# Another table of places for the order of all instructions in a graph stack of four layers

## The chip, the cores and the metric

The kernel runs on one core of a Trainium2 chip. The metric is the device time of one launch in microseconds (us). A core has engines with an instruction stream each: PE (TensorE, matrix products into PSUM), DVE (VectorE), ACT (ScalarE), POOL (GpSimd) and SP (SyncE, which here issues nearly all DMAs). [...]

## The reference

`x` is 32 graphs of 512 nodes with 256 features, `adj` their 0/1 adjacency. Four layers follow each other, each on a normalised and clipped copy of x. Everything is float32.

```python
h = relu(layernorm(x)); x = x + gat4(h, adj)       # layer 0: 4 heads of 64, exp(leaky(e_i + e_j)), softmax over j
h = relu(layernorm(x)); x = x + gat1(h, adj)       # layer 1: 1 head of 256, softmax over i
h = relu(layernorm(x)); x = x + edge(h, adj)       # layer 2: scores (h * a_0) h^T, leaky, softmax
h = relu(layernorm(x)); x = x + transformer(h, adj)  # layer 3: 8 heads of 32, Wo, norm, 256-1024-256 net, norm
```

## The kernel before

**One list of jobs for each graph.** `quick_path` (line 325) walks through the 32 graphs. For each it makes two loads (`adj`, `x`), then `masks`, `layer0` to `layer3`. These functions issue nothing yet: each operation is handed to a plan (`plan.dve`, `plan.act`, `plan.matmuls`, `plan.dma`), which appends a job. There are 497 jobs to a graph, in the same order for every graph.

**The table decides the order.** A job's place is the graph's number times 100,000 plus the table's entry for that job's position in the list (`put`, line 150). `carry_out` (line 178) sorts the jobs of all graphs by place and issues them in that order. On each engine this order is kept; across engines the data decide. The entries are keys for a sort and no times.

```python
place = self.number * ROUND + self.table[self.at] if self.place is None else self.place
```

Entries reach to almost 500,000, so five graphs are under way at once. I call the leading digit of an entry its stage (0 to 4), and round r the jobs with places from r times 100,000: in round r graph r is in stage 0, graph r-1 in stage 1, and so on to graph r-4 in stage 4. Rounds 0 to 3 fill this pipeline, rounds 4 to 31 are full, rounds 32 to 35 drain it.

**What the stages hold.** Roughly: stage 0 has loads, the mask, layer 0's normalisation and first products (`ps_t`, `ps_wh`, `ps_sp`); stage 1 layer 0's four heads (`p` on DVE, `ps_o` on PE); stage 2 layer 1 and most of layer 2; stage 3 the end of layer 2 and layer 3's `ps_qk`, `ps_v` and attention; stage 4 layer 3's `ps_wo` and feed-forward net (`ps_f`).

**The attention of layer 3** (lines 695 to 724) goes in eight steps, two groups of four heads by four blocks of keys. A step is: four score products (`ps_s`, contraction over 32 rows), two exponentials on ACT (`p<-ps_s`), one multiplication by the mask on DVE (`p<-p,m`), and eight products into 32 columns each (`ps_ct` for the context, `ps_to` for the row sums). The buffer `p3` holds two steps.

**Buffers.** A tile takes the slot of its kind that was used longest ago. PSUM has two slots for layers 0 to 2 and the last net (`ps_a`), two for layer 3 (`ps_b`), and one each for `ps_ct` and `ps_to`. `p` has 6 slots, `mT` 3. The layer weights are loaded on POOL's queue behind the load of the first x (`plan.load`, line 238), at the place that `plan.aside(max(PLACES[:2]) + 1)` gives.

Of the kernel before, what the change touches and what calls it, by code (L numbers as in the profile page):

```python
# [56 lines left out]
class Part:  # L57


    def __init__(self, home, rows, index, steps=()):  # L60
        self.home, self.rows, self.index, self.steps = home, rows, index, steps
# [61 lines left out]
class Plan:  # L123
# [8 lines left out]

    def __init__(self, tc, table):
        self.tc, self.nc, self.table = tc, tc.nc, table
        self.jobs = []

    def graph(self, number):

# [136 lines left out]
def width(args):  # L275
# [4 lines left out]

ROUND = 100000
PLACES = [
    19807, 0, 43241, 57619, 64598, 73580, 81389, 88138, 134062, 235662, 143142, 287307, 285553, 232853, 15635,
    15811, 28841, 27985, 23993, 15811, 30374, 30229, 32369, 32370, 32370, 32446, 32844, 48496, 34324, 44230,
    44177, 46695, 46041, 50344, 54161, 54792, 54792, 54792, 51041, 51777, 57310, 57310, 57310, 57738, 57738,
    57832, 57739, 58104, 61341, 61341, 67966, 61898, 61898, 67567, 69254, 72469, 69482, 77323, 74000, 76325,
    79818, 78024, 78024, 80713, 80713, 80714, 82170, 88138, 93984, 93675, 88138, 100363, 101562, 103520,
    103520, 103520, 103520, 99026, 98456, 107942, 108892, 114155, 115978, 115979, 116955, 117229, 118109,
    112967, 112266, 118498, 118106, 122333, 124077, 124856, 124856, 126720, 126720, 130323, 126361, 126793,
    124647, 132760, 132760, 132760, 132760, 134221, 134221, 134221, 134221, 134221, 134727, 134221, 156322,  # L290
    140191, 134912, 142057, 169073, 157725, 170057, 172384, 201862, 202787, 205641, 207797, 208539, 176096,
    208573, 211867, 216328, 218484, 218484, 219056, 219056, 219056, 219056, 219056, 218484, 218484, 218484,
    218484, 218485, 227052, 227119, 228253, 219613, 219613, 220424, 224906, 224906, 228631, 223683, 224122,
    224122, 229201, 229201, 232797, 231582, 232020, 232794, 233389, 243904, 244480, 249048, 254893, 242125,
    242231, 243790, 254173, 237217, 238008, 241105, 245079, 237839, 238826, 242604, 256707, 257566, 258334,
    259006, 259006, 259006, 259519, 259519, 259519, 259519, 259519, 392456, 255868, 267182, 259006, 259006,
    259892, 259665, 259006, 259006, 259892, 259665, 266786, 266786, 268621, 269711, 273176, 302934, 273176,
    273176, 273176, 277010, 277447, 281097, 281097, 281195, 281196, 281196, 281682, 281682, 281682, 281682,
    281683, 281196, 281683, 282840, 282840, 284327, 283254, 286775, 286821, 286821, 287236, 288036, 287335,
    282681, 282681, 283122, 282681, 284575, 293213, 293213, 295654, 291792, 291574, 293905, 297714, 297584,  # L300
    297714, 298819, 298819, 297714, 287489, 287489, 290592, 290231, 298206, 300033, 308229, 310297, 310297,
    303799, 303799, 303799, 305379, 305380, 306132, 308300, 312883, 316207, 394029, 437737, 327509, 328548,
    327753, 325228, 328998, 329876, 332238, 330645, 332238, 332502, 332502, 332608, 332717, 364575, 332717,
    332717, 332717, 332717, 332717, 338203, 340406, 340406, 340406, 340407, 340407, 340905, 341309, 341309,
    352943, 347109, 352371, 352371, 353369, 353369, 353417, 354661, 356381, 356381, 356381, 357144, 357399,
    346769, 348254, 348493, 351248, 352029, 352189, 352199, 352199, 352554, 359237, 359237, 359237, 359237,
    364034, 360298, 360301, 360448, 365688, 377452, 366095, 368722, 368232, 374829, 379739, 379671, 380891,
    379672, 382370, 383191, 386847, 392755, 392755, 387818, 392756, 395158, 396303, 407857, 382331, 382331,
    382615, 382634, 388690, 385894, 388773, 389314, 389314, 394131, 390806, 394842, 396200, 401293, 405927,
    398693, 403322, 398865, 403593, 407530, 409955, 410479, 412422, 412422, 408793, 409986, 423530, 354795,  # L310
    408893, 410479, 418263, 418263, 418263, 419191, 419191, 419191, 419191, 419128, 417119, 437177, 437347,
    419191, 420203, 420203, 420203, 420203, 420721, 420203, 420203, 421199, 422452, 422452, 423633, 423633,
    432009, 424134, 424134, 424718, 424718, 424759, 425616, 425916, 425916, 425916, 425916, 426698, 426841,
    426841, 426970, 427475, 430939, 430939, 427202, 428368, 428368, 428368, 429763, 429360, 431209, 431243,
    432263, 432263, 432291, 432540, 430070, 430071, 430071, 430071, 430446, 430071, 431829, 432836, 432836,
    435307, 436332, 440746, 435945, 435945, 436252, 436626, 436626, 437927, 444318, 444318, 444811, 444811,
    444811, 445291, 445291, 445291, 445291, 445447, 445572, 436110, 437653, 437653, 437653, 437653, 437653,
    438770, 440843, 440843, 440843, 440843, 440843, 440872, 442233, 442446, 442446, 442446, 445600, 445600,
    442446, 442446, 445601, 445601, 442446, 442704, 446845, 449648, 449758, 449759, 449759, 454221, 449777,
    450699, 450699, 450699, 450699, 450699, 450699, 491710,  # L320
]


# [993 lines left out]
```

## Time and profile before

| | us |
|---|---|
| median of 3 runs (3751.09 to 3758.95) | 3752.26 |
| the profiled execution | 3758.1 |
| its span, first to last instruction | 3756.2 |
| PE busy in the span | 3635.0 (97%) |
| DVE busy | 2732.6 (73%) |
| ACT busy | 1803.8 (48%) |
| one full round (graph to graph) | 111.37 |

In the profile all planned operations have one line each for their helper: L214 for DVE and ACT, L259 for PE's matmuls, L257 for its transposes. So groups are told apart by tile names. Names have their numbers left out: `ps_o` is the head product of layer 0 (65 columns), the product of layer 1 (256) and that of layer 2 (257); `ps_f` are both products of the net. Every float32 matmul is two instructions on PE, a transpose is one.

### The profile page before, as it was taken

What the parts mean: (1) busy time and instruction counts of PE and PEld (TensorE: products, weight loads), DVE (VectorE), ACT (ScalarE), POOL (GpSimd) and SP (SyncE); (2) the same over time, 40 slices, a digit from 0 to 9 for tenths busy, and PEclk for the clock granted to TensorE, in tenths of its full rate; (3) what the DMA queues carried; (4) which work ended last, traced back from release to release, by engine and by line L of the source; (5) the groups of instructions that cost most, each with busy time, mean ns of one, the idle gap of its engine ahead of it and who ended that gap; (6) DMA issues with size and microseconds to landing.
All of it is one profiled execution on the core that took longest, in us unless ns stands there. A gap on an engine that the chain in (4) does not pass through costs nothing.

```text
span 3756.2 us, 51774 instructions
## 1 busy us (share of the span) xinstructions
PE 3635.0 (97%) x19974; PEld 2366.4 (63%) x19974; DVE 2732.6 (73%) x6267; ACT 1803.8 (48%) x3393; POOL 11.1 (0%) x25
## 2 busy tenths in 40 slices
PE   4799999999999999999999999999999999999996
PEld 4666766666766666666666666666666666666553
DVE  4577777877777777777787777787777777777653
ACT  1245445555444555444555544555544455544543
POOL 1000000000000000000000000000000000000000
PEclk7599999999999999999999999999999999999998
DMA  4111111111111111011111111111111111100000
GB/s 120 57 32 33 36 49 46 43 42 36 29 49 46 43 49 36 23 47 47 49 43 38 40 29 49 46 43 49 29 29 49 46 43 49 38 29 27 15 9 11
DMA packets 152349, 152.72 MB, mean 41 GB/s; under 512 B 87840, under 2 KB 122144, under 8 KB 148000
## 3 DMA queue, kind: packets, MB, share of 16 engines
q1 hardware_dynamic: 149632, 144.35, 13.8%
q0 software_dynamic: 1216, 3.94, 0.3%
q8 instruction: 159, 2.61, 0.3%
q10 hardware_dynamic: 1248, 1.05, 0.1%
q14 instruction: 94, 0.77, 0.1%
HBM read 114.57 MB, written 17.96 MB: 35 GB/s over the span
## 4 chain that ended last, share of the span: by engine, by line
PE 95%; DVE 3%; ACT 1%; DMA 1%; issue 1%; SPq 0%; ACTq 0%; DVEq 0%
PE ps_o L259 25%; PE ps_f L259 24%; PE ps_s L259 7%; PE ps_ct L259 7%; PE ps_wh L259 6%; PE ps_qk L259 6%; PE ps_to L259 6%; PE ps_e L259 4%; PE ps_t L257 4%; PE ps_v L259 3%; PE ps_wo L259 3%; DVE p L214 1%; PE ps_y L257 1%; DVE st L214 0%; DMA mT<-m 0%
## 5 line engine op out<-in xcount | busy, mean ns | idle before, releaser
L259 PE MATMUL ps_o<-wh,p 128*128 128x65 f32 (+1 forms) x5120 | 750.5, 303 | 30.2 <-DVE p L214 24.6
L259 PEld LDWEIGHTS ps_o<-wh,p 128*128 128x128 f32 x5120 | 705.6, 200 | 102.7 <-issue 60.5
L214 DVE TENSOR_TENSOR p<-p,m 128x2048 f32<-128x2048 f32 x256 | 582.7, 2286 | 29.7 <-ACT p L214 29.6
L214 ACT ACTIVATE p<-ps_s 128x1024 f32<-128x1024 f32 x512 | 501.2, 1022 | 208.1 <-PE ps_s L259 205.3
L259 PE MATMUL ps_f<-tT,ff_t 128*128 128x512 f32 x1024 | 462.7, 602 | 1.7 <-ACT tT L214 1.7
L259 PE MATMUL ps_f<-ff_t,f 128*128 128x256 f32 x2048 | 461.0, 379 | 0.0
L259 PEld LDWEIGHTS ps_f<-ff_t,f 128*128 128x128 f32 x2048 | 381.9, 190 | 64.0 <-issue 15.3
L214 DVE SCALAR_TENSOR_TENSOR p<-rows,rt,mT 128x512 f32<-128x512 f32 x512 | 370.1, 735 | 16.7 <-DMA mT<-m 16.7
L214 ACT ACTIVATE h<-x,shift,rstd 128x256 f32<-128x256 f32 x512 | 268.6, 595 | 152.8 <-PE ps_o L259 106.3
L259 PEld LDWEIGHTS ps_f<-tT,ff_t 128*128 128x128 f32 x1024 | 189.4, 192 | 229.3 <-issue 188.7
L259 PE MATMUL ps_s<-qk 32*128 32x512 f32 x2048 | 294.2, 640 | 1.3 <-ACT qk L214 0.8
L259 PE MATMUL ps_ct<-p,v 128*32 128x512 f32 x2048 | 272.0, 603 | 9.3 <-DVE p L214 6.3
L214 ACT ACTIVATE f<-ps_f,ff1b_c 128x512 f32<-128x512 f32 x256 | 164.8, 682 | 235.7 <-PE ps_f L259 235.7
L259 PE MATMUL ps_to<-p,ones 128*32 128x512 f32 x2048 | 266.6, 592 | 0.0
L259 PE MATMUL ps_qk<-h3T,wqkv_t 128*128 128x512 f32 x512 | 239.1, 594 | 0.0
L259 PE MATMUL ps_o<-h,p 128*128 128x257 f32 x1024 | 239.0, 385 | 0.0
L259 PEld LDWEIGHTS ps_o<-h,p 128*128 128x128 f32 x1024 | 190.1, 191 | 51.5 <-issue 26.0
L214 DVE BATCH_NORM_STATS2 st<-x 128x6 f32<-128x256 f32 x512 | 195.6, 415 | 6.8 <-DMA x<-in_x_dram 4.7
L214 ACT ACTIVATE rstd<-mv,eps 128x4 f32<-128x4 f32 x192 | 56.4, 294 | 298.6 <-DVE mv L214 286.0
L257 PE MATMUL ps_t<-ident,h 128*128 128x128 f32 x1024 | 172.6, 281 | 25.0 <-ACT h L214 17.6
L259 PEld LDWEIGHTS ps_s<-qk 32*128 32x128 f32 x2048 | 81.3, 182 | 164.6 <-ACT y L214 78.0
L257 PEld LDWEIGHTS ps_t<-ident,h 128*128 128x128 f32 x1024 | 130.8, 145 | 85.2 <-issue 52.3
(131 smaller groups left out, 4322.9 us busy)
## 6 DMA issues: line engine op xcount, KB each, us to landing
adj<-in_adj_dram SPq DMA_DIRECT2D x32, 1024.0 KB
rows<-rows_d SPq DMA_DIRECT2D x32, 1024.0 KB
x<-in_x_dram SPq DMA_DIRECT2D x32, 512.0 KB
rows<-rows_d SPq DMA_DIRECT2D x32, 512.0 KB
out_dram<-y SPq DMA_DIRECT2D x32, 512.0 KB
inv<-in_d SPq DMA_DIRECT2D x32, 256.0 KB
ff_t<-in_L_gnn_W_dram POOLq DMA_DIRECT2D x2, 1024.0 KB, 12.5
mT<-m SPq DMA_TRANSPOSE x128
```

The costliest lines, as they stand in the source:

```text
L214: return [getattr(unit, method)(*map(real, args), **{k: real(v) for k, v in kw.items()})]
L257: made.append(self.nc.tensor.transpose(*map(real, c)))
L259: made.append(self.nc.tensor.matmul(*map(real, c[:3]), start=c[3], stop=c[4]))
```

## The change

The table `PLACES` (lines 282 to 321) is replaced; 496 of its 497 entries differ. The plan's constructor also gets `number = None`, which changes no instruction. The jobs, their operands, their buffers' kinds and slot counts are the same.

```diff
-        self.jobs = []
+        self.jobs, self.number = [], None
...
 PLACES = [
-    19807, 0, 43241, 57619, 64598, 73580, 81389, 88138, 134062, 235662, 143142, 287307, 285553, 232853, 15635,
...
-    450699, 450699, 450699, 450699, 450699, 450699, 491710,
+    4941, 0, 45989, 55878, 52736, 53088, 65883, 75806, 126827, 257141, 153885, 318759, 211656, 217633, 19570,
...
+    442345, 444396, 453835, 453835, 478083,
 ]
```

What moves, read from the two tables:

- 39 jobs change their stage. Layer 0's first head (four `ps_o` jobs, their release on DVE and three further `p`) goes from stage 1 to 0. The root and shift of layer 1's normalisation go from 2 to 1, three of the four `ps_o` jobs of layer 2 from 3 to 2, the last two attention steps from 4 to 3. Three small DVE jobs move on by a stage or two.
- The cyclic order of a full round stays alike. PE before: first head, two layer-2 `ps_o`, `ps_ct` of steps 7 and 8, two `ps_o`, `ps_wo` with the second head inside. After: three matmul jobs of the first head, `ps_y`, the fourth, one layer-2 `ps_o`, `ps_ct` of steps 7 and 8, three `ps_o`, the second head, `ps_wo`.
- Layer 1's `ps_wh`: before, eight jobs in five runs between single jobs of the third head; after, four jobs, then the whole third head, then two, one and one between the transposes of layer 3's first norm.
- Between those transposes (`ps_t<-ident,n`) and the first `ps_f` PE had two `ps_wh` jobs; now it has two jobs of the fourth head.
- In attention, `ps_t` of layer 2 moves from behind `ps_ct` of step 3 to in front of it, and `ps_e` and `ps_y` of layer 2 stand in other gaps.
- On DVE, the four `p` of a head: before, two of them stood behind the release of the head in front (second, third and fourth head alike); now two, three and two do, and in the second and fourth head the first one that PE uses is the last one made.
- On SP, three of the four mask transposes (`mT<-m`) now stand in front of the store of layer 0's row (`rows_d`), before two did. The load of adj stands directly behind that of x, now by 4,941 places, before by 19,807; nothing else of SP lies between in either table for the first graph.

## The prediction

> **What bounds the kernel now.** I read the page first: span, busy shares, chain.
>
> ```profile
> span 3756.2 us, 51774 instructions
> PE 3635.0 (97%) x19974; PEld 2366.4 (63%) x19974; DVE 2732.6 (73%) x6267; ACT 1803.8 (48%) x3393; POOL 11.1 (0%) x25
> PEclk7599999999999999999999999999999999999998
> PE 95%; DVE 3%; ACT 1%; DMA 1%; issue 1%; SPq 0%; ACTq 0%; DVEq 0%
> ```
>
> PE carries the end: 95% of the chain. Its clock is low in the first two slices only. Next the busy times by round. I found the round from the first head's product, which comes back every 111.37 us. Columns: stretch, length, then busy time and count of PE, PEld, DVE, ACT, POOL; clock; DMA.
>
> ```profile
> 96.00:138.40 42.40, 37.72 (x153) 34.19 (x153) 16.21 (x40) 4.86 (x14) 0.00 (x0) 0.50 0.10 36
> 184.50:273.60 89.10, 84.55 (x475) 55.97 (x476) 64.17 (x153) 42.16 (x80) 0.00 (x0) 0.90 0.09 25
> 273.60:384.98 111.38, 111.38 (x627) 72.40 (x626) 84.96 (x196) 56.22 (x107) 0.00 (x0) 1.00 0.15 42
> 3280.79:3392.16 111.37, 111.37 (x626) 72.38 (x626) 84.96 (x196) 56.20 (x107) 0.00 (x0) 1.00 0.15 42
> 3392.16:3500.20 108.04, 106.60 (x601) 69.02 (x600) 76.77 (x171) 51.07 (x90) 0.00 (x0) 1.00 0.04 14
> 3500.20:3598.30 98.10, 94.22 (x473) 55.60 (x472) 61.76 (x136) 49.87 (x89) 0.00 (x0) 0.98 0.05 14
> 3598.30:3694.30 96.00, 82.41 (x405) 43.40 (x407) 48.62 (x83) 37.45 (x55) 0.00 (x0) 0.95 0.04 12
> 3694.30:3756.20 61.90, 38.33 (x138) 23.31 (x130) 18.38 (x45) 12.25 (x23) 0.00 (x0) 0.83 0.03 10
> ```
>
> The span is 273.6 of fill, 28 full rounds of 111.37 (3118.6), and 364.0 of drain. In full rounds PE is busy all the time, first to last; the waits of PE between 240 and 3380 are none at all. So a table cannot shorten a full round by removing idle time. What it can change is how tightly PE's own instructions follow each other, whether a new wait comes up, and the ends: 32 rounds of 111.37 are 3563.8, so 192 us are spent on fill and drain.
>
> To see slack inside a busy PE I read start to start in the timeline of one full round.
>
> ```profile
> 1075.30 1.04 PE L259 MATMUL ps_wh<-w_t,h1T 128*128 128x258 f32 x4
> 1076.17 1.00 PE L259 MATMUL ps_o<-wh,p 128*128 128x65 f32 x8
> ...
> 1082.36 1.04 PE L259 MATMUL ps_wh<-w_t,h1T 128*128 128x258 f32 x4
> 1083.39 8.85 PE L259 MATMUL ps_f<-tT,ff_t 128*128 128x512 f32 x20
> ...
> 1128.54 1.05 PE L259 MATMUL ps_wh<-w_t,h0T 128*128 128x264 f32 x4
> 1129.43 1.89 PE L259 MATMUL ps_o<-wh,p 128*128 128x256 f32 x8
> ...
> 1137.04 1.16 PE L259 MATMUL ps_wh<-w_t,h0T 128*128 128x264 f32 x4
> 1138.13 1.07 PE L259 MATMUL ps_ct<-p,v 128*32 128x512 f32 x8
> ```
>
> Four `ps_wh<-w_t,h1T` take 0.87 to the next start, but 1.03 in front of `ps_f`: a hidden wait of 0.16 for `tT`; the first `ps_f` behind it is 0.105 late as well, so 0.27 in all. Four `ps_wh<-w_t,h0T` take 0.89 among whole-array products, but 1.09 between `ps_s` (32 rows) and `ps_ct` (32 columns): each change of the array's shape costs 0.09 to 0.11 (0.055 from `ps_s` to a transpose).
>
> At the ends PE waits for these, most of all:
>
> ```profile
> PE ps_o L259 <- DVE p L214: 24.6, 9, 10.0
> PE ps_t L257 <- ACT n L214: 12.5, 3, 5.0
> ```
>
> [...] graph 1's first normalisation starts at 73.8 only when DVE has done graph 0's update of x. [...]
>
> **The change part by part.** Nothing is added or removed; every cost is one of order.
>
> *Full rounds, shape changes.* I counted them in both cyclic orders: 24 before, 25 after. `ps_s` to transpose and back to `ps_ct` takes the place of `ps_s` directly in front of `ps_ct` (which was free): +0.055 + 0.093 = +0.15 a round. The runs of 65-column products are six in both, no change.
>
> *Full rounds, the hidden wait.* Between the last layer-3 transpose and the first `ps_f` PE now has two head jobs (0.84 + 0.89) where it had two `ps_wh` (0.87). ACT's two `tT` were 0.27 short, now they have 0.86 more: -0.27. Cover in front of these transposes stays 6.1 (four `ps_wh`, four head jobs, two `ps_wh`: 1.7 + 3.5 + 0.9; before 6.05), against a chain from `ps_wo` through the norm of 5.0 (the longest wait in the last row above).
>
> *Full rounds, a new wait?* The tightest place that I find is attention step 6. From the end of its scores, two exponentials (1022 ns each) and the mask multiplication (2286) take 4.3, with two hand-overs some 4.7. PE meanwhile does three `ps_y` (0.4), step 5's `ps_ct`/`ps_to` (1.85), step 7's scores (1.07) and four `ps_e` (1.5): 4.8, before 5.1. DVE must also be on time: between the end of step 3's mask multiplication and that of step 8's it has 23 us of work by its starts, PE 24.3. So 0.1 is left, if nothing is late. Bounds: 0, and 0.6 a round (one more DVE job, 0.67 as `p` shows by its starts, in front). I take 0.07.
>
> Sum of a full round: +0.15 - 0.27 + 0.07 = -0.05; times 28: **-1.4**.
>
> *Fill, SP.* In rounds 0 and 1 the first `p` waits last for a transpose `mT<-m` (16.7 in three waits), issued behind `rows`. Three transposes instead of two are now in front, so `rows` lands last. One transpose's issue is 1.2; I take half of it, 0.6, twice: -1.2 (bounds 0 and -2.4).
>
> *Fill, heads of round 1.* PE works at half clock, one head 6.8, and DVE releases the head (0.6) and makes the next `p` (0.67 each). The new order puts one more `p` in front of the first product, the two late ones of the second head last, three instead of two behind the release for the third, and none of the extra statistics for the fourth: +0.7 + 1.3 - 0.9, about +1.0.
>
> *Fill, round 2.* Layer 1's `ps_sp` now has half a head in front (its wait was 1.1): -1.0. And the clock: layer 1's eight transposes and four `ps_wh` come as one run of about 5.5 us at half clock, where before two `ps_wh` and then head jobs came. [...] the trace's stretches at full clock are 10.2 long as at 155.2, and about 14 us of half-speed products run in 7: between 0 and -7. [...] I take half, -3.5.
>
> *Drain.* The product count that is missing in each round shifts between rounds but its sum is the same. Round 34's attention, alone on PE, has the same sequence, and the tail's chain too. New: with the first head gone, step 8's `ps_ct` has 3.9 of cover (`ps_y`, one `ps_o`, `ps_ct`) for the chain of 4.7, in rounds 32 and 33, where before two `ps_o` gave 5.5: +0.8 twice, less small gains: **+1.5**.
>
> Sum: -1.4 - 1.2 + 1.0 - 1.0 - 3.5 + 1.5 = -4.6. Against the profiled execution 3758.1 - 4.6 = 3753.5; that one ran 5.8 over the median of the runs shown, so against the median 3752.3 - 4.6 = **3747.7**.
>
> What hides the moved DVE and ACT work is PE itself: DVE is 85 and ACT 56 of 111. Without that cover the cost is the rival below.
>
> **Rivals.**
>
> *Faster, the early rounds at full clock.* As at 192.7 in the trace, full clock can hold for over 20 us [...]. Then round 2 gains its 7, and round 3 loses its relapse (216.6 to 226.8 at half, some 4): another -7.5 to my sum, and if step 6 waits nothing, -2 more: 3738. For it: the longer dense run. Against it: a dense run of four `ps_wh` at 126.5 to 130.2 released nothing.
>
> *Slower, DVE as the bound of attention.* If DVE comes late to step 6 by 0.6 in each full round, 28 times: +16.8 instead of +2, so 3762.5. It decides from 0.38 a round, where all other terms are eaten up and 7.5 are lost. For it: 0.1 of slack against 23 of dense DVE work. Against it: five places with 0.5 or less of slack give no idle PE today.
>
> *No effect.* Full rounds are all PE, the ends cancel: 3752.
>
> **From this to numbers.** A measurement of this kernel tells about 0.2% (7.5 us) from no change. Forecast 0.45 (3740 to 3756; 0.13 of it faster, 0.31 the same, 0.01 slower), faster rival 0.30, slower rival 0.20, no effect 0.05. That makes 0.43, 0.36, 0.21. The range leaves out half of each rival's far side: 3732 to 3764. Cases of both signs hold half of the chance, so the forecast's own range stands here: 3740 to 3756.
>
> **What would show it.** A full round of 111.2 to 111.5; `ps_f` behind head jobs without the 0.16; no PE wait between 250 and 3380. The clock above 0.5 in round 2, or not. Step 8's `ps_ct` waiting about 0.8 in rounds 32 and 33. Wrong it would be with repeated waits of `ps_ct` for DVE's `p` in full rounds, or with a fill changed by over 10 us through a chain that I took as equal.

## The result, and the profile after

| | before | after |
|---|---|---|
| median of 7 runs each, us | 3757.42 (3750.60 to 3759.99) | 3740.05 (3735.43 to 3741.35) |
| the profiled execution, us | 3758.1 | 3739.68 |
| its span, us | 3756.2 | 3737.7 |

The changed kernel is faster by 0.41%: the ratio is 0.9959, with a 95% interval of 0.9949 to 0.9969. The predicted time was 3747.7; the sum behind it said -4.6 us, and the span of the traced executions fell by 18.5. About half of all executions of the kernel before on record take 3748 to 3754 us at a mean granted clock of 0.977 to 0.98, the others, the traced one (3758.1) among them, 3756 to 3761 at 0.975 to 0.977, so up to 8 of the 18.5 us lie between executions of one and the same kernel.

The page of the kernel after: span, busy times, granted clock by slice, and the chain that ended last by engine.

```profile
span 3737.7 us, 51923 instructions
PE 3619.6 (97%) x19974; PEld 2361.0 (63%) x19974; DVE 2743.3 (73%) x6267; ACT 1814.9 (49%) x3393; POOL 11.1 (0%) x25
PEclk6699999999999999999999999999999999999998
PE 94%; DVE 3%; ACT 1%; DMA 1%; issue 0%; SPq 0%; ACTq 0%; DVEq 0%
```

PE still carries the end, with as many instructions as before, and is busy 15.4 us less. The busy times by stretch follow, of the kernel after (columns as in the prediction): graph 1's heads, then graph 2's first head to graph 3's, then two full rounds.

```profile
98.22:130.10 31.88, 28.79 (x153) 26.20 (x153) 14.73 (x36) 4.97 (x13) 0.00 (x0) 0.66 0.04 14
174.10:258.74 84.64, 82.12 (x472) 54.06 (x473) 64.56 (x152) 42.99 (x82) 0.00 (x0) 0.94 0.09 26
258.74:369.79 111.05, 111.05 (x626) 72.54 (x625) 85.28 (x196) 56.59 (x107) 0.00 (x0) 1.00 0.14 42
3257.89:3368.95 111.06, 111.06 (x626) 72.55 (x625) 85.28 (x196) 56.59 (x107) 0.00 (x0) 1.00 0.14 42
```

Three things moved. A full round takes 111.05, not 111.37. Graph 1's heads are the same 153 instructions, but at a clock of 0.66 and in 31.9 us, where they took 42.4 at 0.50. And the full rounds start some 15 us earlier (273.6 and 258.7).

I cut both spans at the start of the first attention scores of graphs 0 and 28, since the rounds between them are full ones:

| part of the span | before | after | difference | predicted |
|---|---|---|---|---|
| fill, to the first scores of graph 0 | 240.23 | 225.54 | -14.7 | -4.7 |
| 28 rounds, to those of graph 28 | 3118.55 | 3110.30 | -8.3 | -1.4 |
| drain, to the end | 397.4 | 401.9 | +4.4 | +1.5 |

All three have the predicted sign, and all three are larger. The experiments ask why.

### The profile page after: what moved, and what is told of

Same layout as the page of the kernel before. It is cut to its first block, busy times and chain, and to the rows that moved or that the text cites. A ratio compares the mean times of both kernels' runs of the same rounds, so it can differ in the third digit from the quotient of the medians.

```text
span 3737.7 us, 51923 instructions
## 1 busy us (share of the span) xinstructions
PE 3619.6 (97%) x19974; PEld 2361.0 (63%) x19974; DVE 2743.3 (73%) x6267; ACT 1814.9 (49%) x3393; POOL 11.1 (0%) x25
## 4 chain that ended last, share of the span: by engine, by line
PE 94%; DVE 3%; ACT 1%; DMA 1%; issue 0%; SPq 0%; ACTq 0%; DVEq 0%
PE ps_o L259 25%; PE ps_f L259 24%; PE ps_s L259 7%; PE ps_ct L259 6%; PE ps_wh L259 6%; PE ps_qk L259 6%; PE ps_to L259 6%; PE ps_t L257 4%; PE ps_e L259 4%; PE ps_v L259 3%; PE ps_wo L259 3%; DVE p L214 2%; PE ps_y L257 1%; DMA rows<-rows_d 1%; ACT p L214 0%
## 5 line engine op out<-in xcount | busy, mean ns | idle before, releaser
L259 PE MATMUL ps_o<-wh,p 128*128 128x65 f32 (+1 forms) x5120 | 736.2, 301 | 30.5 <-DVE p L214 27.5
L259 PEld LDWEIGHTS ps_o<-wh,p 128*128 128x128 f32 x5120 | 690.7, 197 | 97.4 <-issue 42.8
L214 DVE TENSOR_TENSOR u<-ps_f,n 128x512 f32<-128x512 f32 x64 | 44.3, 692 | 238.3 <-PE ps_f L259 238.3
L214 DVE BATCH_NORM_STATS2 st<-x 128x6 f32<-128x256 f32 x512 | 204.3, 415 | 9.2 <-DMA x<-in_x_dram 4.8
L257 PEld LDWEIGHTS ps_t<-ident,h 128*128 128x128 f32 x1024 | 121.3, 143 | 101.1 <-issue 52.4
```

Source lines behind the costliest of these rows:

```text
L214: return [getattr(unit, method)(*map(real, args), **{k: real(v) for k, v in kw.items()})]
L257: made.append(self.nc.tensor.transpose(*map(real, c)))
L259: made.append(self.nc.tensor.matmul(*map(real, c[:3]), start=c[3], stop=c[4]))
```

## The full rounds

**The hidden wait.** The timeline of PE after, around the first `ps_f`:

```profile
3065.40 0.60 PE L257 MATMUL ps_t<-ident,n 128*128 128x128 f32 x4
3065.84 1.90 PE L259 MATMUL ps_o<-wh,p 128*128 128x65 f32 x16
3067.57 12.23 PE L259 MATMUL ps_f<-tT,ff_t 128*128 128x512 f32 x28
```

From the head jobs to `ps_f` it is 1.73 us, 0.84 and 0.89, so nothing is hidden there now. I then compared, job by job, the median time from a PE job's start to the next one's in 16 full rounds of both kernels. The job in front of `ps_f` lost 0.158 and the first `ps_f` 0.104, together the predicted 0.26. To see whether that is what a round gained, one run puts the wait back into the new table and another takes it out of the old one.

*Run `wait_back`.*

```diff
+MOVED = {b: {101: 118504, 102: 118505, 141: 216500, 142: 216501, 143: 216900, 154: 216910} for b in range(32)}
...
     for b in range(B):
+        plan.table = list(PLACES)
+        for at, place in MOVED.get(b, {}).items():
+            plan.table[at] = place
         plan.graph(b)
```

Jobs 101 and 102 are the head jobs, 141 to 143 the pair of `ps_wh` and its copy, 154 a small ACT job that needs this copy.

> The new table, but in all graphs the two head jobs between the transposes of layer 3's norm and the first ps_f go behind the second pair of ps_f's, and the last pair of layer 1's ps_wh with its copy stands there instead, as in the old table. Theory (0.27 of the 0.32 that a full round gained is the hidden wait for tT): full rounds of 111.31 to 111.36, 7 to 9 us over the changed kernel. Rival (the round gained by closer packed 65-column products and shape changes elsewhere): rounds of 111.0 to 111.1, within 2 us of the changed kernel.

Its timeline of PE at the same place:

```profile
1178.37 1.03 PE L257 MATMUL ps_t<-ident,n 128*128 128x128 f32 x8
1179.25 1.04 PE L259 MATMUL ps_wh<-w_t,h1T 128*128 128x258 f32 x4
1180.28 4.56 PE L259 MATMUL ps_f<-tT,ff_t 128*128 128x512 f32 x10
```

The pair of `ps_wh` takes 1.03 again. Most rounds take 111.31, 0.26 more than after, as the theory says (7.3 us in 28 rounds), and job by job the 0.26 sit at this place alone. The median is 3743.83 (ratio to the kernel before 0.9969, 0.9959 to 0.998), 3.8 over the changed kernel's; the span of the traced execution is 9.4 over it, with three rounds that were longer by 0.9 to 1.5 for a reason shown below. The rival is out; the size in the medians is under the expected 7 to 9.

*Run `wait_off`* takes the old table and moves one pair of `ps_wh` behind the transposes. (From here on `...` stands for the lines that hand the moved places to the plan, as in `wait_back`.)

```diff
+MOVED = {b: {147: 227120, 148: 227121} for b in range(32)}
...
```

> The old table with one edit for all graphs: the pair of ps_wh that stood in front of the transposes of layer 3's norm goes behind the other pair, in front of the first ps_f, so that PE has four ps_wh jobs (1.73 us) while ACT makes tT, not two. Nothing else moves. Theory (0.27 a round is the hidden wait for tT): full rounds of 111.08 to 111.15 instead of 111.37 and 6 to 8 us under the kernel before, if the 5.15 us that are left in front of the transposes still cover their chain of 5.0. Rival (that wait was not worth a time, or another comes up in its place): within 2 us of the kernel before.

It took 3772.4 us, 0.38% over the kernel before (1.0024 to 1.0052), and rounds of 111.87: the theory was wrong, and of the rival the second half came, another wait in its place, but larger than it had it. The timeline of PE in this run, and then of the kernel before:

```profile
3097.44 1.85 PE L257 MATMUL ps_t<-ident,n 128*128 128x128 f32 x8
3099.13 1.91 PE L259 MATMUL ps_wh<-w_t,h1T 128*128 128x258 f32 x8
3100.88 8.74 PE L259 MATMUL ps_f<-tT,ff_t 128*128 128x512 f32 x20
```

```profile
3086.26 1.04 PE L257 MATMUL ps_t<-ident,n 128*128 128x128 f32 x8
3087.14 1.04 PE L259 MATMUL ps_wh<-w_t,h1T 128*128 128x258 f32 x4
3088.17 8.85 PE L259 MATMUL ps_f<-tT,ff_t 128*128 128x512 f32 x20
```

The wait for `tT` did go: the two pairs of `ps_wh` take 1.75, and the last `ps_wh` and the first `ps_f` lost 0.157 and 0.106. But the eight transposes now take 1.69 to the next start and not 0.88: the third, the fifth and the seventh come 0.2 late each, with small pauses beside them. The chain of 5.0 ends with the first quarter of `n` only; these three wait for the others, which come about half a us apart. So in the old order a round could not have its 0.26 by moving `ps_wh`; the new table gets it because the cover in front of the transposes stays and other work, the head jobs, stands behind them.

**The other part of a round.** The same comparison gives the rest of the -0.32. Visible shape changes (a pause of 0.09 to 0.11 where the array goes over between whole, 32 rows and 32 columns) are 16 before and 17 after: +0.09, predicted +0.15. Not predicted: a wait of 0.10 between layer 2's transposes, which stood directly behind `ps_sp` in the old order, is gone; and of the pauses of 0.056 that runs of 65-column products and of transposes show, there is one fewer. Together about -0.15. I take these from the trace; no run tested them.

**The new wait at step 6.** The prediction put 0.07 a round on it. No full round after shows a wait of `ps_ct`. One run shows how near it is.

*Run `p_later`.* Some rounds after are longer than 111.05, and the trace shows why. PE and DVE in such a round, taken from the timeline of the run `dense_cut` (below), where it is largest:

```profile
3243.90 0.75 DVE L214 SCALAR_TENSOR_TENSOR p<-rows,rt,mT 128x512 f32<-128x512 f32 x1 [1.82 <-DMA rows<-rows_d]
3244.57 0.68 DVE L214 TENSOR_TENSOR y<-y,y 128x512 f32<-128x512 f32 x1
3245.31 0.55 PE L257 MATMUL ps_y<-ident,y 128*128 128x128 f32 x3 [1.43 <-DVE y L214]
```

With its first head in stage 0, a graph's first `p` follows its row's way to memory and back by some 9 us. When the row is late, DVE stands at this `p`, layer 2's `y` stands behind it, and PE waits for `y`. So I moved that `p` behind `y` and the two `p2`.

```diff
+MOVED = {b: {69: 79200} for b in range(32)}
...
```

> The new table, with the first p of the first head, which DVE makes as soon as the row has come back from memory, placed behind layer 2's y and its two p2 in all graphs. Theory (in some rounds of the new table the row's transfer is late and DVE holds layer 2's y behind that p, so that PE waits 0.1 to 1.5 us for ps_y): all full rounds take 111.05 to 111.08, none 111.15 or more, and the time is 0.5 to 3 us under the changed kernel. Rival (the late rounds come from something else on DVE): the same odd rounds appear, within 0.5 us of the changed kernel.

It went the other way: 3752.67 us, the time of the kernel before (ratio 0.9994, 0.9988 to 1.0001). The odd rounds did go, all 28 take 111.52 or 111.53. But each is 0.47 longer, all of it in front of one job, `ps_ct` of step 6. The waits of PE from 560 to 3300, this run and then the kernel after:

```profile
PE ps_ct L259 <- DVE p L214: 10.1, 25, 0.4
```

```profile
PE ps_y L257 <- DVE y L214: 0.4, 2, 0.2
```

One `p` of 0.67 (start to start) in front of the next mask multiplication makes attention wait 0.47 in every round. So about 0.2 us (0.67 less 0.47) is the margin of the new order there, and the mechanism of the rival *slower* is real; the table just doesn't reach it. The late row costs much less: 0.8 us in all in the profiled execution after.

## The fill

The milestones of the fill, from the traces of the kernels before and after and of three runs that follow:

| start of, us | before | after | dense_more | warm_fill | warm_both |
|---|---|---|---|---|---|
| graph 1's first head | 96.0 | 98.2 | 95.8 | 88.5 | 89.2 |
| end of graph 1's heads | 138.4 | 130.1 | 128.0 | 117.0 | 113.2 |
| graph 2's first head | 184.6 | 174.1 | 174.3 | 161.0 | 157.5 |
| graph 0's first scores | 240.2 | 225.5 | 230.0 | 212.4 | 207.4 |

After is 2.3 late at first, gains 10.6 while graph 1's heads run, 2.2 up to graph 2's first head, and 4.2 behind it. The clock goes with it. By the trace's record it is full after from 119.96 to 133.61, with breaks from 147.27 on, and from 184.82 until the drain; before, it is half from 90.31 to 155.16, and after a full stretch from 192.71 it falls back once more, from 216.60 to 226.84. The timeline of PE after, where the first of these stretches begins:

```profile
115.22 2.12 PE L257 MATMUL ps_t<-ident,h 128*128 128x128 f32 x8
117.12 3.40 PE L259 MATMUL ps_wh<-w_t,h1T 128*128 128x258 f32 x8
120.36 3.68 PE L259 MATMUL ps_o<-wh,p 128*128 128x65 f32 x32
```

The dense run of 5.1 us that the prediction named is there. But does the clock cause the gain, or go with it?

*Run `dense_cut`* breaks that run in the new table, for graph 0 alone.

```diff
+MOVED = {0: {150: 209306, 151: 209391}, 1: {92: 109390, 93: 109392}}
...
```

> The new table, but for graph 0 alone the third and fourth of layer 1's ps_wh jobs go between the head jobs of graph 1, as the old table has them. Theory (eight transposes and four ps_wh in one run release the clock near 120 us, and the fill gains through it): the clock stays at 0.5 until about 145, the first attention scores of graph 0 start 6 to 11 us later than 225.5, and the time is 6 to 11 us over the changed kernel. Rival (the fill gains by its order, with fewer waits, and the clock only follows): within 2 us of the changed kernel.

It took 3738.45 us (ratio 0.9956, 0.9942 to 0.9969), level with the changed kernel. The number is the rival's, but the edit didn't do what it should: the clock was full all the same, from 117.40 on, behind the eight transposes and the two `ps_wh` left in the run (3.9 us). So this run tells nothing between the two, except that full clock came here without four `ps_wh`.

*Run `dense_more`* goes the other way: the old table, with graph 0's run made dense.

```diff
+MOVED = {0: {150: 219614, 151: 219615}}
...
+    for place, n in ((218500, 1), (219500, 1)):
+        plan.aside(place)
+        more = new("ps_b", "ps_more", [P, D + 2 * H0])
+        for _ in range(n):
+            plan.matmuls(0.445, (more, ident, w0_t[:, 0], True, True))
```

> The old table, with graph 0's layer-1 products alone made one run without a gap and without a 65-column product: the third and fourth ps_wh directly behind the first two, and two further products of 264 columns, whose result nobody reads, in the two gaps between the transposes and ps_wh. This adds work of about 1 us. Theory (the fill gains because such a run releases the clock): clock 1.0 from 117 to 122 on instead of from 155, graph 0's first attention scores 6 to 12 us earlier than 240.2, and the time 6 to 12 us under the kernel before. Rival (the fill gains by its order, the clock only goes with it): 0 to 2 us over the kernel before.

More work, and faster: 3748.69 us, ratio 0.9981 (0.9973 to 0.9989). The medians lie 8.4 us apart and the traced spans 10.2; against the half of the executions of the kernel before that already ran at the higher clock it is only some 4 us. The busy times in the last 3.41 us at half clock and the first 3.41 at full, and then over all of graph 1's heads (this run, clock in the column behind POOL):

```profile
110.90:114.31 3.41, 3.41 (x16) 3.04 (x16) 1.54 (x4) 0.59 (x1) 0.00 (x0) 0.50 0.00 0
114.31:117.72 3.41, 3.03 (x18) 2.42 (x16) 2.35 (x5) 0.37 (x1) 0.00 (x0) 1.00 0.00 0
95.80:128.00 32.20, 28.45 (x157) 26.01 (x157) 16.21 (x40) 4.86 (x14) 0.00 (x0) 0.71 0.11 40
```

The clock is full 40.9 us earlier than before, and the first scores come 10.2 earlier, with the old order in everything else. This shows the clock as the cause of the gain in graph 1's heads (32.2 us here, 31.9 after, 42.4 before): of the 10.2 us, 9.3 are PE's shorter busy time (28.45, before 37.72) and only 0.9 are idle time, which the moved `ps_wh` could have changed by order alone. It also shows what it is not: here the fall-back to half clock is still there, from 206.47 to 216.71, and the further 4.2 us behind graph 2's first head don't come, so they are the new order's own. After has no such fall-back behind graph 2's heads; that this is what the 4.2 are is argued.

*Runs `extra` and `warm_fill`* ask whether earlier rounds, too, lose time to the half clock. Both are the new table with further products as above, in time that PE stood idle; `extra` has 10 in front of graph 0's and graph 1's first head, `warm_fill` 20 there and 4 in front of later heads.

```diff
+    for b, at, n in ((0, 71, 20), (0, 81, 4), (0, 91, 4), (0, 101, 4), (1, 71, 20), (1, 81, 4)):
+        plan.aside(b * ROUND + PLACES[at])
+        more = new("ps_b", "ps_more", [P, D + 2 * H0])
+        for _ in range(n):
+            plan.matmuls(0.445, (more, ident, w0_t[:, 0], True, True))
```

> The new table, and ten further products of 264 columns, whose result nobody reads, in front of the first head of graph 0 and again of graph 1, where PE stands idle for 9.4 and 9.6 us. Theory (in rounds 0 and 1 PE at half clock is on the path that sets the end): the clock is 1.0 when the first heads begin, each of these two heads takes 3.5 to 5 us instead of 8, and the time is 3 to 10 us under the changed kernel. Rival (65-column products let the clock fall again at once, or DVE's p sets the pace of the heads): within 2 us of the changed kernel.

`extra` took 3739.0 us (0.9954, 0.994 to 0.9967), no gain. By its busy times the ten products ran at full clock already, in front of graph 1's head, but PE then stood idle for 5.6 us (the second stretch is the last 4.7 of them):

```profile
88.00:93.40 5.40, 4.50 (x21) 3.50 (x19) 0.68 (x3) 0.20 (x1) 0.00 (x0) 1.00 0.39 102
93.40:98.10 4.70, 0.00 (x0) 0.00 (x0) 2.16 (x5) 0.00 (x0) 0.00 (x0) 0.72 1.03 373
98.10:115.10 17.00, 14.17 (x64) 13.83 (x65) 6.12 (x13) 2.08 (x4) 0.00 (x0) 0.50 0.07 28
```

So the clock had fallen before the head began, and the run doesn't decide what it was meant to.

> The new table with further products of 264 columns, whose result nobody reads, in the idle time of PE in rounds 0 and 1: 20 in front of the first head of graphs 0 and 1, so that PE works right up to the head, 4 in front of the other heads of graph 0 and of the second head of graph 1. Theory (the clock holds through the heads once it is released and PE has no gap; half clock there is on the path): heads of graph 0 and 1 take about 4 us instead of 8, time 8 to 20 us under the changed kernel. Rival (products of 65 columns let the clock fall even from full): clock 0.5 within 10 us of each first head, time within 3 us of the changed kernel.

With PE at work almost up to the heads it took 3723.93 us (0.9912, 0.99 to 0.9925), 16 us under the changed kernel by the medians and 12.4 by the traced spans. The busy times of this run up to graph 1's heads and in them, and then of the kernel after:

```profile
25.00:88.50 63.50, 51.64 (x260) 43.18 (x258) 28.38 (x71) 7.47 (x20) 0.00 (x0) 0.84 0.32 93
88.50:117.00 28.50, 26.79 (x161) 24.03 (x161) 14.67 (x37) 4.97 (x13) 0.00 (x0) 0.82 0.04 16
```

```profile
25.00:98.22 73.22, 39.11 (x159) 34.62 (x158) 28.75 (x72) 7.79 (x23) 0.00 (x0) 0.57 0.26 81
98.22:130.10 31.88, 28.79 (x153) 26.20 (x153) 14.73 (x36) 4.97 (x13) 0.00 (x0) 0.66 0.04 14
```

DVE's and ACT's work is nearly the same in both; PE gets 101 records more up to graph 1's heads and ends them 13 us sooner. Half clock in rounds 0 and 1 was on the path. But the clock did not hold as the theory had it: it fell 3.7 us after graph 0's first head began (for 6.8 us) and 1.6 us after graph 1's (for 10.2), which is the rival's sign, though not its time. Why was not shown: `warm_both` (below) has the same further products in the fill, and there the clock is 1.00 through graph 1's heads.

## The drain, and two tables in one kernel

*Runs `fill_new` and `drain_old`* were meant to split fill and drain from the rounds, with a table for each part. Where graphs of both tables are under way, some jobs find no free slot; in these two runs such a job waits its turn, through a change of `carry_out` that is not shown here.

```diff
     for b in range(B):
+        plan.table = list(OTHER if b < 4 else PLACES)
         plan.graph(b)
```

(`fill_new`, with the old table as `PLACES`; `drain_old` has the new one there and the condition `b > 27`.)

> Graphs 0 to 3 take the new table, graphs 4 to 31 the old one. Theory (the change's 18.5 us are three separate sums: -14.7 in the fill, -0.32 in each full round, +5 in the drain): only the fill is new, so the first attention scores of graph 0 start near 225.5 instead of 240.2, full rounds take 111.37 and the time is 13 to 17 us under that of the kernel before. Rival (the early start is lent and given back when the pipeline is full, the gain sits in the full rounds): 0 to 4 us under it.

> The new table, but graphs 28 to 31 take the old one. Theory (the drain of the new table costs 4.5 to 5 us more, by its order): 4 to 6 us under the changed kernel, near 3734. Rival (half of this drain difference is a stretch at half clock that fell in the last attention by chance): 1 to 3 us under it. If the mixed rounds 28 to 31 wait, less than that.

They took 3851.92 us (1.026, 1.0244 to 1.0275) and 3840.26 us (1.0231, 1.0217 to 1.0245): some 100 us lost, as no theory had it. The first scores of graph 0, and a stretch in the rounds of both tables, from the timeline and from the busy times of `fill_new`:

```profile
225.81 1.14 PE L283 MATMUL ps_s<-qk 32*128 32x512 f32 x8
```

```profile
374.40:798.00 423.60, 367.86 (x1834) 234.89 (x1826) 250.49 (x576) 160.54 (x306) 0.00 (x0) 0.91 0.12 33
```

The fill is that of the new table to 0.3 us, so its gain needs nothing of the rounds behind it. The loss is in the mixed rounds, which take 114, 141, 146 and 153 us from first scores to first scores, before 111.37 comes back: in the stretch shown PE is idle for 56 of 424 us, and the clock falls to a mean of 0.91. Two orders that are each free of waits don't make one when mixed. On the drain `drain_old` says nothing.

For the drain's +4.4 there are the traces alone. Its busy times from the first scores of graph 29 to those of graph 30, and from those of graph 31 to the end, of the kernel before and then after, with the waits for `tT` in the whole run:

```profile
3468.38:3566.51 98.13, 94.24 (x472) 55.63 (x471) 61.91 (x140) 49.90 (x88) 0.00 (x0) 0.98 0.05 15
3663.32:3756.20 92.88, 62.39 (x314) 29.87 (x314) 37.20 (x57) 29.32 (x42) 0.00 (x0) 0.89 0.03 10
PE ps_f L259 <- ACT tT L214: 1.7, 2, 0.9
```

```profile
3445.13:3545.74 100.61, 95.20 (x472) 55.79 (x471) 62.79 (x142) 49.78 (x88) 0.00 (x0) 0.98 0.04 14
3643.07:3737.70 94.63, 64.70 (x314) 30.11 (x314) 38.23 (x56) 28.90 (x41) 0.00 (x0) 0.86 0.03 10
PE ps_f L259 <- ACT tT L214: 2.6, 3, 0.9
```

The first of these parts is 2.5 us longer after: the first `ps_f` of graph 29 waits 0.9 visibly there, as the head jobs in front of it are gone, and a `ps_y` waits 0.4 for `y`, as another does a round later. The last part is 1.8 longer, with a further stretch of 6.8 us at half clock in graph 31's attention, from 3645.93. The predicted wait of step 8 in rounds 32 and 33 didn't come.

*Run `warm_drain`* tests the clock's part: the new table, and further products in PE's waits of the last two rounds.

```diff
+    for b, at, n in ((30, 405, 11), (31, 317, 3), (31, 322, 2), (31, 331, 2), (31, 349, 2), (31, 359, 2), (31, 364, 2), (31, 374, 5), (31, 405, 11)):
...
```

> The new table with further products of 264 columns, whose result nobody reads, in the idle time of PE in the last two rounds: 11 in the wait for n in front of the transposes of graphs 30 and 31, and 2 to 5 in each wait of graph 31's attention and ps_wo. Theory (the waits of the drain let the clock fall, and the products behind them run at half speed): no half clock between 3590 and 3720, 8 to 11 us under the changed kernel. Rival (the half-clock stretches lie beside waits for ACT and DVE anyway): within 2 us of the changed kernel.

It took 3734.22 us (0.9939, 0.9928 to 0.9951), 5.8 under the changed kernel, with no half clock from 3508 to 3722. The busy times of the last part, this run and then the kernel after:

```profile
3586.00:3733.00 147.00, 127.09 (x577) 75.96 (x576) 61.26 (x120) 47.52 (x76) 0.00 (x0) 0.96 0.03 11
```

```profile
3583.50:3737.70 154.20, 117.03 (x502) 64.64 (x498) 61.38 (x120) 47.97 (x76) 0.00 (x0) 0.88 0.03 10
```

With PE's waits filled, the half clock is gone and the time falls, as the theory has it; the expectation put the gain too high. Each of the two places with transposes and `ps_f` behind a wait gained 2.5 us, where I had expected more than 4: of some 10 us at half clock PE stood idle or waited for 3.6, and the transposes go at the pace of `n` also at full clock (eight in 1.92).

*Run `warm_all`* adds the moved `p` to both, *run `warm_both`* leaves it out.

> The edits of the three runs before together. Theory: their sums add, 15 to 30 us under the changed kernel. If the heads of the fill don't hold the clock: 8 to 12 us under it, all from the drain.

> The new table with the further products of the fill and of the drain, and without the moved p. Theory (fill and drain gain apart from each other, 13 and 5.6 us of span; full rounds keep 111.05): 3716 to 3722 us, 17 to 21 us under the changed kernel. If the moved p was of use after all, over 3724.

`warm_all` took 3731.36 us (0.9937, 0.9924 to 0.995): its fill is 16 us shorter than the changed kernel's, but the moved `p` took 0.47 in each round, as in `p_later`. So it missed its 15 to 30. `warm_both` took 3715.73 us (3713.66 to 3716.49), ratio 0.9892 (0.9875 to 0.991) to the kernel before, the best of all, and 24 us under the changed kernel by the medians, a little more than expected; in graph 1's heads the clock held this time (1.00 from 89.2 to 113.2). Its page:

```profile
span 3713.9 us, 52306 instructions
PE 3634.5 (98%) x20166; PEld 2375.6 (64%) x20166; DVE 2742.6 (74%) x6267; ACT 1814.3 (49%) x3393; POOL 11.1 (0%) x25
PEclk9899999999999999999999999999999999999999
```

192 PE records more than after, whose results nobody reads, and 23.8 us of span less.

## Why the prediction was right and wrong

The direction, the bound (PE, by order and not by idle time) and the three places were right; the sizes were too small. That 3740.05 still lies in the range, at its lower edge of 3740, is luck: the sum said -4.6, the medians moved by 17.4, and the rival *faster* (3738) was nearer. By the prediction's own steps:

- *Full rounds, the hidden wait*, -0.27: right. 0.26 in the comparison by jobs, and 0.26 when `wait_back` restored it.
- *Full rounds, shape changes*, +0.15: too high. The step into a transpose, priced at 0.055, costs nothing in the median; +0.09.
- *Full rounds, a new wait*, 0.07 at step 6: none there. `p_later` shows 0.2 us of margin. The rival *slower* needed 0.6 us of DVE work more in front; with 0.67 it appeared, at 0.47 a round.
- *Sum of a full round*, -0.05: this is one failed sum. +0.22 was put against -0.27, of which only 0.09 came, and 0.15 of small pauses that went weren't seen, because only the place in front of `ps_f` was read start to start in the prediction. -0.32 in the median, 28 times, less 0.8 for late rows.
- *Fill, SP*, -1.2: the order of landing was right (in the fill the first `p` now waits last for `rows<-rows_d`, 15.6 us in all, before for `mT<-m`, 16.4), so the wait is 0.8 shorter, but no head starts earlier for it. *Heads of round 1*, +1.0: together these two were -0.2, and graph 1's first head is 2.3 late. 1.7 of it are there at graph 0's fourth head (62.2, now 63.9): by the order of DVE, the `p` that stands in front of a head in its new place costs in graph 0's heads too, which the step left out.
- *Fill, round 2*, half of a bound between 0 and -7: the step that failed most. Full clock came, and by the traces of `dense_more` and of the kernel before it is worth 10.2 us, more than the bound itself: the full stretch is 13.65 long and not 10.2, and it takes in all of the second half of graph 1's heads. Halving a bound for a thing that either happens or not gave a number that belongs to neither case. The rival *faster* (3738) had the early full clock, the relapse in round 3 that goes (4 us, measured 4.2), and nearly the time. The fill changed by more than the 10 us that were to speak against the prediction, though through the clock and not through a chain taken as equal.
- *Drain*, step 8's waits, +1.5: the wrong wait. What came was the wait for `tT` in front of graph 29's `ps_f`, and the clock.
- *No PE wait between 250 and 3380*, nearly: two waits of 0.2 for `y` (from 560 to 3300), from the late row of the moved head, which no step had.
- *A sum of the rival slower*: it was to decide from 0.38 a round. The other terms (6.6) and 7.5 lost make 14.1 us, and that is 0.50 a round.

## What to carry to other kernels

Where PE waits at the ends of a pipeline, look at the granted clock of the stretch behind the wait: products whose results nobody reads, put into the wait so that they last right up to the real work, gave 24 us here, more than the new order of all the work did (17 by the medians). Price a hidden wait by what stands between producer and consumer on the waiting engine, and before moving cover to one place check the wait that it leaves. And read a whole round start to start, job by job, before summing small changes: the pauses that nobody asked about were worth more than half of the one that was.

## What the runs showed of the hardware

PE can be busy all the time and stay at half clock. The busy times of the kernel before in three stretches of 3.41 us, with two 65-column head jobs and one or two `ps_wh` in each:

```profile
117.61:121.03 3.42, 3.42 (x15) 3.14 (x13) 0.00 (x0) 0.37 (x1) 0.00 (x0) 0.50 0.00 0
121.03:124.44 3.41, 3.41 (x16) 3.22 (x15) 0.00 (x0) 0.37 (x1) 0.00 (x0) 0.50 0.00 0
124.44:127.85 3.41, 3.41 (x14) 3.15 (x14) 1.10 (x3) 0.00 (x0) 0.00 (x0) 0.50 0.00 0
```

And of the kernel after, two stretches and the one in which the clock is full:

```profile
113.13:116.55 3.42, 3.42 (x17) 3.08 (x17) 0.85 (x3) 0.00 (x0) 0.00 (x0) 0.50 0.00 0
116.55:119.96 3.41, 3.41 (x11) 2.46 (x10) 3.41 (x6) 0.96 (x2) 0.00 (x0) 0.50 0.00 0
119.96:123.37 3.41, 3.41 (x31) 3.35 (x29) 0.03 (x1) 0.38 (x1) 0.00 (x0) 1.00 0.00 0
```

The five at half clock are all 100% busy. The first four were followed by half clock, the fifth by full, so busy time as the profile shows it does not part them. In the fifth, transposes and `ps_wh` fill the time, with 11 PE records where the others have 14 to 17. But their number does not part them either: the stretch of `dense_more` from 110.90 to 114.31 (in the section on the fill) has 16 and was followed by full clock. Which property of the work or of its time decides was not shown, as no run was built to test it. Three more readings belong here:

- Head products alone, at half clock: in the kernel before, from 100.55 to 103.96, PE was busy for 3.41 of 3.41 us with them at 0.50, and in the 3.41 us behind it the clock was 0.50 too.
- The four `ps_wh` at 126.5 of the kernel before, which the prediction held against its rival *faster*, ran at 0.50, and the clock stayed there up to 155.16. Why full clock followed the dense runs of `dense_cut`, `dense_more` and the kernel after and not this one was not shown.
- Graph 1's heads, with the same further products in front of them and between them, took two courses: in `warm_fill` the mean clock from 88.5 to 117.0 was 0.82, in `warm_both` it was 1.00 from 89.2 to 113.2:

```profile
89.20:113.20 24.00, 22.04 (x161) 19.58 (x161) 14.64 (x36) 4.97 (x13) 0.00 (x0) 1.00 0.06 22
```

A nearly equal order can also take another course of the clock. In the profile of `dense_cut` it stays full from 165.19 to 202.73, where the changed kernel's profile has half clock from 174.58 to 184.82, and the first scores come at 220.2 instead of 225.5. What decides this was not shown.
